# Two-layer graph network on one core: the normed inputs turned to channels by DMA, as planes of half words

## The chip, the cores and the metric

The kernel runs on one core of a Trainium2 chip. The metric is the device time of one execution in microseconds (us), the median of the runs shown; less is better. The engines are named as the profile names them: PE is TensorE (PEld its weight loads), DVE is VectorE, ACT is ScalarE, POOL is GpSimd, SP is the engine from which most DMAs are issued. "L312" is line 312 of the kernel before.

## What is computed

64 graphs of 256 nodes and 256 channels go through two residual layers, each with a layer norm and a ReLU ahead of it.

```python
# layer 0: three steps of message passing with one GRU cell
h = relu(layernorm(x))
A = (adj != 0)
for i in range(3):
    m = h @ weight[i]
    aggr = einsum('bst,bsd->btd', A, m)
    h = gru_cell(aggr, h, w_ih, w_hh, b_ih, b_hh)   # three gates of 256 channels
x = x + h
# layer 1: attention with 4 heads of 64 channels over the same graph
h = relu(layernorm(x))
v = h @ W.T + b
logits = leaky_relu(l_src[:, :, None, :] + l_dst[:, None, :, :], 0.2)
logits = where(adj == 1, logits, -9e15)
x = x + softmax(logits, axis=2) @ v
```

## The kernel before

**Tiling.** The graphs are taken in 32 pairs. A pair has 512 nodes, as four row tiles of 128 nodes (`R` = 4) by 256 channels (`D`). The state of layer 0 is kept with channels on the partitions: `hT_a` is 128 x (2 x 512), two halves of the channels (`KD` = 2) by 512 nodes. So the normed input `xn_a`, which has nodes on the partitions, has to be turned before layer 0, and `xn_b` before layer 1.

**How it is turned.** `plan_relu_T` (L360) does it for both layers: for each half of the channels PE transposes four 128 x 128 blocks against the identity into one PSUM bank (L370, tiles `pt_a` and `pt_b`), and ACT copies the bank out with a ReLU (L371). `plan_norm` (L329) makes `xn`: statistics on DVE (L339, L340), the inverse deviation on POOL (L346), and `xn` = (x - mean) * rstd on DVE (L351).

**The order of the work.** Nothing is scheduled by a planner that knows costs. Each piece of work is put by hand at a tick and one of three phases (STEP, READY, REST) with `at(tick, phase, pair, fn)`; the program is emitted tick by tick, phase by phase, the later pair first. Each engine then runs its own instructions strictly in that order. A step of the GRU takes 6 ticks (`SUB`); pair p starts at tick 18p (`APART`); its three steps stand at its ticks 0, 12 and 24. The gaps are filled by the steps of the neighbours, so that every stretch of 6 ticks holds one step of one pair. Over 18 ticks three such stretches follow each other and then repeat. They are called stages here, by the ticks modulo 18: stage B is ticks 0 to 5, stage C ticks 6 to 11, stage A ticks 12 to 17.

**Inside one step** (`Step`, L384) PE runs, in this order: `qa`, the sums over neighbours `pa` (L440), small blocks `qa`, `qb` (L418), and blocks of eight matmuls each (L312): `pc`, `p`, `pd`, `pc`, `pd`, `pe`, `pn`, `pd`, `pn`. DVE makes operands between them: L453, L461, L462, L468, L474, then L479 (writes `pe` from the first `pd`), L495 (`first_n`, writes the start of each of the two `pn` banks, on which PE then accumulates), L489 (reads the second `pd`, after which PE may add the third), and at the step's end, after POOL's L510, the new state with L527 and L528.

**Beside the steps** stand, at fixed ticks of each pair:

- `xn_a` (statistics at -14 and -13, result at -7), its turning at -4 and -3, and `hNhi_a`, `hNlo_a` (L742, L746), which split the ReLU of `xn_a` in two parts for the sums over neighbours;
- `edge` at -1 and `noedge` at 35 (L733, L800), made from the adjacency, `noedge` also written to DRAM;
- `xn_b` at 32 to 34, its turning at 35 and 36, the values `pv` (PE L820, DVE L824, which adds the bias `b_val`) at 37 and 38;
- `score_rows` (L853) at 39: a small transpose, four small DMAs to DRAM, and two loads `drow` that spread the scores over all partitions;
- `linked` (L863) at 36: a DMA transpose of `noedge` out of DRAM, issued on SP; from it ACT fills the logits `zz` (L872) at 38 to 41;
- `add_rows` (L878) at 43, 44 and 56, 57: DMAs issued on POOL that add rows onto `zz`;
- the row maxima (L899) at 43 to 50, the leaky ReLU on ACT (L919) at 48 to 55, the exponentials (L934) at 60 to 63, the products `po` (PE L542) with their division (DVE L551, L553) and residual (POOL L558) at 62 to 65, and the write of the result (L531) at 66.

SP issues, in order: the write of an old pair's result, the loads of x and of both uses of the adjacency, the small score rows, `drow`, `noedge` to DRAM, and `linked`. Buffers are rings by tag (`BUFS`, L100): a load waits until the old content of its buffer has been used.

Of the kernel before, what the change touches and what calls it, by code (L numbers as in the profile page):

```python
# [9 lines left out]
F32 = mybir.dt.float32  # L10
F32R = mybir.dt.float32r
BF16 = mybir.dt.bfloat16
I32 = mybir.dt.int32
AF = mybir.ActivationFunctionType
ALU = mybir.AluOpType
# [11 lines left out]
def gated_gnn_then_gat_kernel(  # L27
# [69 lines left out]
    def bank(name):  # L97
        return ps_m.tile([P, 512], F32, tag="mm", name=name)

    BUFS = {  # L100
        "x": 5, "adj": 2, "edge": 2, "noedge": 2, "hT_a": 2, "xn": 2, "val": 2, "row": 4, "zz": 4, "o": 2,
    }

    def buf(tag, shape, name, dtype=F32):
# [7 lines left out]
    def load_adj(p, name):  # L112
        at = buf("adj", [P, R, N], f"{name}_{p}", I32)
        nc.sync.dma_start(at, adj_rows[ts(p, T), :].rearrange("(r q) t -> q r t", q=P))
        return at

    def load_x(p):
        xt = buf("x", [P, R, D], f"x_{p}")
        nc.sync.dma_start(xt, x_rows[ts(p, T), :].rearrange("(r q) d -> q r d", q=P))
        return xt  # L120
# [13 lines left out]
    def load_square(tag, name, src):  # L134
        y = buf(tag, [P, KD, D], name)
        nc.sync.dma_start(y, src.rearrange("(k q) e -> q k e", q=P))
        return y
# [5 lines left out]
    hh_T = [buf("row", [P, G * P], f"hh_T_{k}") for k in range(KD)]  # L143
    w_msgs = [load_square("Z", "w_msg_0", weight[0])]
    ih_nat = load_gates("ih", w_ih)
    w_msgs += [load_square("row", f"w_msg_{l}", weight[l]) for l in range(1, L)]
    w_nat = load_square("zz", "w_nat", W)
    bi = const.tile([P, G], F32, name="bi")
    bh = const.tile([P, G], F32, name="bh")
# [176 lines left out]
    def at(tick, phase, p, fn):  # L326
        plan.setdefault(tick, ([], [], []))[phase].append((-p, fn))

    def plan_norm(src, name, p, ticks):  # L329

        v = {}

        def stats(r0):
            def fn():
                if not v:
                    v["st"] = small.tile([P, R, 6], F32, tag="st", name=f"st_{name}")
                    v["mv"] = small.tile([P, R, 2], F32, tag="mv", name=f"mv_{name}")
                for r in (r0, r0 + 1):
                    nc.vector.bn_stats(v["st"][:, r, :], src()[:, r, :])  # L339
                    nc.vector.bn_aggr(v["mv"][:, r, :], v["st"][:, r, :])  # L340
            return fn

        def deviation():
            rstd = v["rstd"] = small.tile([P, R], F32, tag="rstd", name=f"rstd_{name}")
            nc.vector.tensor_scalar_add(rstd, v["mv"][:, :, 1], EPS)
            nc.gpsimd.tensor_tensor(rstd, rstd, mhalf, ALU.pow)  # L346

        def result():
            xn = v["xn"] = buf("xn", [P, R, D], f"xn_{name}")
            for r in range(R):  # L350
                nc.vector.tensor_scalar(  # L351
                    xn[:, r, :], src()[:, r, :], v["mv"][:, r, 0:1], v["rstd"][:, r : r + 1],
                    op0=ALU.subtract, op1=ALU.mult,
                )

        for t, fn in zip(ticks, (stats(0), stats(2), deviation, result)):
            at(t, READY, p, fn)
        return v

    def plan_relu_T(v, tag, name, p, ticks):  # L360

        w = {}

        def fn(k):
            def go():
                if not w:
                    w["hT"] = buf(tag, [P, KD, T], f"hT_{name}")
                pt = bank(f"pt_{name}_{k}")
                for r in range(R):
                    nc.tensor.transpose(pt[:, ts(r, P)], v["xn"][:, r, ts(k, P)], ident)  # L370
                nc.scalar.activation(w["hT"][:, k, :], pt, AF.Relu)  # L371
            return go

        for k, t in enumerate(ticks):
            at(t, REST, p, fn(k))
        return w

    def by_c(y):
# [331 lines left out]
    def plan_pair(p):  # L710
# [5 lines left out]
        def ready(t, fn):  # L716
            at(t0 + t, READY, p, fn)
# [4 lines left out]
        def rest(t, fn):  # L722
            at(t0 + t, REST, p, fn)


        if p == 0:
            v["x"], v["adj"] = first
        else:
            rest(-20, lambda: v.update(x=load_x(p), adj=load_adj(p, "adj")))

        def to_edge():
            v["edge"] = buf("edge", [P, R, N], f"edge_{p}", F32R)
            nc.vector.tensor_scalar(v["edge"], v["adj"], 0.0, None, op0=ALU.not_equal)  # L733

        xn_a = plan_norm(lambda: v["x"], f"a{p}", p, [t0 - 14, t0 - 13, t0 - 13, t0 - 7])
        ready(-1 if p else -2.5, to_edge)
        h = plan_relu_T(xn_a, "hT_a", f"a{p}", p, [t0 - 4, t0 - 3])


        def first_hi():  # L740
# [66 lines left out]
        if last:  # L807
            plan_tail(t0, p, v, g, lambda i: turn_back(L - 1, i), residual)
            return
        xn_b = plan_norm(lambda: v["x"], f"b{p}", p, [t0 + 32, t0 + 33, t0 + 33, t0 + 34])  # L810
        hb = plan_relu_T(xn_b, "hT_b", f"b{p}", p, [t0 + 35, t0 + 36])

        def values(r0):
            def fn():
                if r0 == 0:
                    v["val"] = buf("val", [P, R, VW], f"val_{p}")
                for r in (r0, r0 + 1):
                    pt = bank(f"pv_{p}_{r}")
                    for k in range(KD):
                        nc.tensor.matmul(  # L820
                            pt[:, :VW], hb["hT"][:, k, ts(r, P)], w_val[:, k, :],
                            start=(k == 0), stop=(k == KD - 1),
                        )
                    nc.vector.tensor_add(v["val"][:, r, :], pt[:, :VW], b_val)  # L824
                if r0 == 0:
                    v["score"] = small.tile([P, R, 2 * H], F32, tag="score", name=f"score_{p}", bufs=2)
                nc.vector.tensor_copy(v["score"][:, r0 : r0 + 2, :], v["val"][:, r0 : r0 + 2, S0:])
            return fn

        rest(37, values(0))  # L830
        rest(38, values(2))

        def as_rows(src, n, what):

# [21 lines left out]
                drow[i] = buf("row", [P, H, N], f"drow_{p}_{i}")  # L856
                nc.sync.dma_start(drow[i].rearrange("q h n -> q (h n)"), on_all(rows["score"][i], H, 1)[:, 0, :])

        rest(39, score_rows)

# [5 lines left out]
        def barred_in(i, j):  # L868
            def fn():
                if j == 0:  # L870
                    logits[i] = buf("zz", [P, KN, H, N], f"zz_{p}_{i}")
                nc.scalar.activation(  # L872
                    logits[i][:, j, :, :], v["link"][:, j : j + 1, ts(i, N)].to_broadcast([P, H, N]),
                    AF.Identity, scale=1 / 16,
                )
            return fn

        def add_rows(i, what):  # L878
            def fn():
                nc.gpsimd.dma_start(  # L880
                    logits[i].rearrange("q j h n -> q j (h n)"), on_all(rows[what][i], 0, KN), accum_op=ALU.add
                )
            return fn

        rest(36, linked)
        ready(38, barred_in(0, 0))
        ready(39, barred_in(0, 1))
        ready(40, barred_in(1, 0))
        ready(41, barred_in(1, 1))
        rest(43, add_rows(0, "score"))  # L890
        rest(44, add_rows(1, "score"))

        def maxima(r, h0):
            def fn():
                if r == 0 and h0 == 0:
                    v["top"] = small.tile([P, R, H], F32, tag="top", name=f"top_{p}", bufs=2)
                for h in (h0, h0 + 1):
                    any_ = buf("any", [P, N], f"any_{p}_{r}_{h}")
                    nc.vector.tensor_tensor_reduce(  # L899
                        any_, drow[r // KN][:, h, :], v["noedge"][:, r, :], 1.0, -3.0e38, ALU.add, ALU.max,  # L900
                        accum_out=v["top"][:, r, h : h + 1],
                    )
            return fn
# [21 lines left out]

        for y in range(R * H // 2):
            r, h0 = divmod(2 * y, H)
            ready(43 + y if not late else 45 + (3 * y) // 8, maxima(r, h0))
            ready(48 + y if not late else 47 + r // KN, leaky(r, h0))
        ready(51 if not late else 47, shift)  # L930
        def exps(i, j):
            def fn():
                zz = logits[i][:, j, :, :]
# [9 lines left out]
        if late:  # L943
            left["rows", p] = shift_rows
            left["add", p] = lambda: [add_rows(i, "topT")() for i in range(PB)]
            for i in range(PB):
                left["exps", p, i] = lambda i=i: [exps(i, j)() for j in range(KN)]
        else:
            rest(52, shift_rows)
            rest(56, add_rows(0, "topT"))  # L950
            rest(57, add_rows(1, "topT"))
            for t, (i, j) in zip((60, 61, 62, 63), ((0, 0), (0, 1), (1, 0), (1, 1))):
                ready(t, exps(i, j))
        if p >= NPAIR - 3:
            for r in range(R):
                left["product", p, r] = lambda r=r: product(p, r, logits[r // KN], v, bank if late else gate_bank)
                left["divided", p, r] = lambda r=r: divided(p, r, v, nc.gpsimd.tensor_add)
            left["write", p] = lambda: write(p, v["x"], 0, R)
        else:
            for r, t in enumerate((62, 63, 64, 65)):  # L960
                rest(t, output(r))
            rest(66, lambda: write(p, v["x"], 0, R))

    for p in range(NPAIR):
        plan_pair(p)
# [52 lines left out]
```

## Time and profile before

| | |
|---|---|
| median of 3 runs | 2533.7 us (2533.55 to 2534.89) |
| profiled execution, its own time | 2540.86 us |
| its span | 2539.1 us |
| granted PE clock, mean | 0.995 |
| busy: PE, PEld, DVE, ACT, POOL | 2514.5, 2246.4, 1824.1, 1466.2, 645.5 us |

The profiled execution took 7.2 us more than the median. A pair takes about 77 us in the steady part (three stages); 32 pairs, a start and a tail make the span. In the lines of the timeline the first column is the start, the second the time from the start to the end of the group; an instruction's recorded duration overlaps its successor a little, so that costs in a row of instructions are best read from start to start.

### The profile page before, as it was taken

To read this page: it belongs to the slowest core of one execution; us is meant where nothing else is said; L and a number is where in the kernel's file an instruction comes from. 1 tells how busy PE (TensorE), PEld (TensorE's weight loads), DVE (VectorE), ACT (ScalarE), POOL (GpSimd) and SP (SyncE) were. 2 spreads that over 40 slices of the span, in tenths; PEclk is the share of its full clock that TensorE was granted. 3 is DMA by queue.
4 is the path that set the end of the run, shared out by engine and by line. 5 is a ranking of instruction groups with operands and counts; after the bars stand their busy time and mean duration, and the time that the engine had idled before them with its cause. 6 is when DMAs were issued, how large, how long until landed. Compare 5 with 4: busy or idle time off the path is not lost.

```text
span 2539.1 us, 38539 instructions
## 1 busy us (share of the span) xinstructions
PE 2514.5 (99%) x13918; PEld 2246.4 (88%) x13918; DVE 1824.1 (72%) x4458; ACT 1466.2 (58%) x3095; POOL 645.5 (25%) x514
## 2 busy tenths in 40 slices
PE   8999999999999999999999999999999999999998
PEld 6888898888889888989888988888988889898887
DVE  5567777677777777776777776777777777767667
ACT  3456565565555565555665655655656656556664
POOL 0122232222222222323232323222222223222221
PEclk9999999999999999999999999999999999999998
DMA  3033434553435544345544444534344544354443
GB/s 94 17 74 88 97 93 108 109 125 92 92 92 117 109 113 99 87 95 117 117 100 93 98 102 109 125 92 100 88 113 109 119 95 93 87 124 110 93 95 89
DMA packets 168223, 251.91 MB, mean 99 GB/s; under 512 B 42896, under 2 KB 128352, under 8 KB 168032
## 3 DMA queue, kind: packets, MB, share of 16 engines
q0 software_dynamic: 33728, 130.03, 26.6%
q1 hardware_dynamic: 132736, 119.41, 16.0%
q8 instruction: 110, 1.80, 0.3%
q14 instruction: 81, 0.66, 0.1%
q10 hardware_dynamic: 1568, 0.01, 0.0%
HBM read 215.62 MB, written 25.67 MB: 95 GB/s over the span
## 4 chain that ended last, share of the span: by engine, by line
PE 97%; DVE 1%; DMA 1%; ACT 1%; issue 0%; POOL 0%; SPq 0%; DVEq 0%
PE pd L312 20%; PE pn L312 13%; PE pc L312 13%; PE po L542 9%; PE pa L440 7%; PE qb L418 6%; PE pe L312 6%; PE p L312 6%; PE qa L418 5%; PE pv L820 4%; PE pback L770 3%; PE pt_a L370 1%; PE pt_b L370 1%; PE pc L238 1%; DVE any L899 0%; DMA hh_nat<-in_L_gnn_w_hh_dram 0%
## 5 line engine op out<-in xcount | busy, mean ns | idle before, releaser
L510 POOL TENSOR_TENSOR R<-hT_a,hn 128x512 f32<-128x512 f32 x191 | 317.8, 1664 | 879.4 <-ACT hn L506 821.5
L312 PE MATMUL pn<-aggr,w_a 128*128 128x256 f32 x1536 | 367.1, 382 | 0.0
L312 PE MATMUL pd<-T,w_a 128*128 128x256 f32 x1536 | 366.3, 381 | 0.0
L312 PEld LDWEIGHTS pn<-aggr,w_a 128*128 128x128 f32 x1536 | 287.0, 190 | 43.1 <-DVE pn L495 6.4
L312 PEld LDWEIGHTS pd<-T,w_a 128*128 128x128 f32 x1536 | 287.9, 191 | 37.6
L542 PEld LDWEIGHTS po<-val,zz 128*128 128x128 f32 x2048 | 250.3, 195 | 4.5
L542 PE MATMUL po<-val,zz 128*128 128x65 f32 x2048 | 247.2, 275 | 0.0
L899 DVE CUSTOM_DVE_ANT_0 any<-drow,noedge 128x256 f32<-128x256 f32 x496 | 236.9, 478 | 9.8 <-DMA drow<-score_dram 1.0
L506 ACT ACTIVATE hn<-pn,bi 128x256 f32<-128x256 f32 x384 | 160.3, 469 | 144.3 <-PE pn L312 144.2
L425 ACT ACTIVATE R<-pc,brz 128x256 f32<-128x256 f32 x192 | 80.5, 470 | 278.5 <-PE pc L312 278.5
L527 DVE SCALAR_TENSOR_TENSOR R<-Z,R 128x512 f32<-128x512 f32 x192 | 131.8, 687 | 147.6 <-POOL R L510 142.8
L558 POOL TENSOR_TENSOR x<-x,o 128x256 f32<-128x256 f32 x124 | 112.0, 904 | 481.6 <-DVE o L553 481.6
L761 DVE TENSOR_TENSOR hNlo<-pback,hNhi 128x512 fp32r<-128x512 f32 x128 | 88.4, 691 | 201.6 <-ACT hNhi L760 201.6
L919 ACT ACTIVATE zz<-zz,val 128x256 f32<-128x256 f32 x496 | 224.9, 509 | 0.0
L495 DVE SCALAR_TENSOR_TENSOR pn<-R,hn 128x512 f32<-128x512 f32 x192 | 142.5, 742 | 93.7 <-ACT hn L421 77.2
L425 ACT ACTIVATE R<-pe,brz 128x256 f32<-128x256 f32 x192 | 80.5, 470 | 185.9 <-PE pe L312 185.9
L528 DVE SCALAR_TENSOR_TENSOR hT_a<-R,hn 128x512 f32<-128x512 f32 x192 | 174.6, 909 | 14.3 <-ACT m5n L446 1.4
L312 PE MATMUL pd<-T,w_h 128*128 128x256 f32 x768 | 181.5, 379 | 0.0
L312 PE MATMUL pc<-aggr,w_a 128*128 128x256 f32 x768 | 181.5, 379 | 0.0
L312 PE MATMUL pe<-aggr,w_a 128*128 128x256 f32 x768 | 181.4, 379 | 0.0
L312 PE MATMUL pc<-hT_a,w_h 128*128 128x256 f32 x768 | 181.4, 379 | 0.0
L312 PE MATMUL p<-T,w_a 128*128 128x256 f32 x768 | 181.4, 379 | 0.0
(176 smaller groups left out, 5258.5 us busy)
## 6 DMA issues: line engine op xcount, KB each, us to landing
zz<-score_dram POOLq DMA_DIRECT2D x62, 1024.0 KB, 11.7
zz<-topT_dram POOLq DMA_DIRECT2D x62, 1024.0 KB, 8.7
adj<-in_adj_dram SPq DMA_DIRECT2D x64, 512.0 KB
drow<-score_dram SPq DMA_DIRECT2D x62, 512.0 KB
x<-in_x_dram SPq DMA_DIRECT2D x32, 512.0 KB
out_dram<-x SPq DMA_DIRECT2D x31, 512.0 KB
noedge_dram<-noedge SPq DMA_DIRECT2D x31, 256.0 KB
score_dram<-score SPq DMA_DIRECT2D x124, 4.0 KB
```

The source lines that it names most:

```text
L312: nc.tensor.matmul(pt[:, ts(c, N)], w[:, k, j * D + c * P : j * D + (c + 1) * P], src[:, k, :], start=start and c == 0 and k == 0, stop=(c ...
L418: nc.tensor.matmul(pt, w_n[:, j, :], src, start=start, stop=True, skip_group_check=True)
L425: nc.scalar.activation(of(dst, i)[:, c, :], src[:, c, :], AF.Tanh, bias=brz[:, g0 + c : g0 + c + 1], scale=0.5)
L440: nc.tensor.matmul(pt[:, ts(i, N)], hN[half][:, i * KN + s, ts(e, P)], edge[:, i * KN + s, :], start=(s == 0 and half == 0), stop=(s == KN ...
L495: nc.vector.scalar_tensor_tensor(by_c(self.bank(f"pn{i}")), of(self.R, i), 1.0, of(self.hn, i), op0=ALU.add, op1=ALU.mult)
L506: nc.scalar.activation(n__[:, c, :], p_n[:, c, :], AF.Tanh, bias=bi[:, 2 * KD + c : 2 * KD + c + 1])
L510: nc.gpsimd.tensor_sub(of(self.R, i), of(self.hT(), i), n__)
L527: nc.vector.scalar_tensor_tensor(d_, of(self.Z, i), 1.0, d_, op0=ALU.add, op1=ALU.mult)
L528: nc.vector.scalar_tensor_tensor(of(self.hT(), i), d_, 0.5, of(self.hn, i), op0=ALU.mult, op1=ALU.add)
L542: nc.tensor.matmul(po[:, ts(h_, VC)], zz[:, j, h_, ts(s, P)], v["val"][:, i * KN + j, ts(h_, VC)], start=(j == 0), stop=(j == KN - 1),)
L899: nc.vector.tensor_tensor_reduce(any_, drow[r // KN][:, h, :], v["noedge"][:, r, :], 1.0, -3.0e38, ALU.add, ALU.max, accum_out=v["top"][:, ...
L919: nc.scalar.activation(zz[:, h, :], zz[:, h, :], AF.Prelu, alpha=ALPHA, bias=v["val"][:, r, S0 + H + h : S0 + H + h + 1],)
```

## The change

Instead of PE and ACT, the DMA engines turn the normed inputs: for layer 0 of the pairs from 2 on, for layer 1 of the pairs 0 to 28. The first pairs, and layer 1 of the last three, keep the old way.

The new `plan_turn` has three parts. `halve` (DVE) copies the 128 x 1024 values as 128 x 2048 half words so that the low and the high half words of a row lie in separate planes (`words`), and SP writes the 512 KB to DRAM. `turn` (SP) reads them back with a DMA transpose of 2-byte elements into `turned`. `join` (DVE) puts the two half words of each value together again in `hT_a` or `hT_b`.

The ReLU has to come ahead of that. For layer 0 ACT applies it to `xn_a` in place. For layer 1 `plan_norm` makes `xn_b` = max(x - mean, 0) without the factor, and the factor `rstd` is multiplied in where the values leave PSUM.

Some ticks move: layer 0's `xn_a` is made at -10 rather than -7, and everything of layer 1 from the values on stands 6 ticks (`later`) later. The loads of x and adjacency go from -20 to -16, and the ring `row` has 2 buffers in place of 4.

```diff
+    def plan_turn(src, tag, name, p, ticks):
+        w = {}
+        def halve():
+            words = buf("words", [P, R, 2, D], f"words_{name}", U16)
+            nc.vector.tensor_copy(words.rearrange("q r w d -> q r d w"), src().bitcast(U16).rearrange("q r (d w) -> q r d w", w=2))
+            w["rows"] = dram.tile([R, P, 2 * D], U16, tag="words", name=f"words_dram_{name}")
+            nc.sync.dma_start(w["rows"].rearrange("r q e -> q r e"), words.rearrange("q r w d -> q r (w d)"))
+        def turn():
+            w["turned"] = buf("turned", [P, 2, KD * T], f"turned_{name}", U16)
+            nc.sync.dma_start_transpose(
+                w["turned"].rearrange("q w (k n) -> q (w k) n", k=KD), w["rows"].rearrange("r q e -> (r q) e")
+            )
+        def join():
+            w["hT"] = buf(tag, [P, KD, T], f"hT_{name}")
+            nc.vector.tensor_copy(
+                flat(w["hT"]).bitcast(U16).rearrange("q (n w) -> q n w", w=2), w["turned"].rearrange("q w n -> q n w")
+            )
+        at(ticks[0], READY, p, halve)
+        at(ticks[1], REST, p, turn)
+        at(ticks[2], READY, p, join)
+        return w
...
-        "x": 5, "adj": 2, "edge": 2, "noedge": 2, "hT_a": 2, "xn": 2, "val": 2, "row": 4, "zz": 4, "o": 2,
+        "x": 5, "adj": 2, "edge": 2, "noedge": 2, "hT_a": 2, "xn": 2, "val": 2, "row": 2, "zz": 4, "o": 2,
...
-            rest(-20, lambda: v.update(x=load_x(p), adj=load_adj(p, "adj")))
+            rest(-16, lambda: v.update(x=load_x(p), adj=load_adj(p, "adj")))
...
-        h = plan_relu_T(xn_a, "hT_a", f"a{p}", p, [t0 - 4, t0 - 3])
+        if dma_a:
+            ready(-10, lambda: nc.scalar.activation(flat(xn_a["xn"]), flat(xn_a["xn"]), AF.Relu))
+            h = plan_turn(lambda: xn_a["xn"], "hT_a", f"a{p}", p, [t0 - 9, t0 - 8, t0 - 3])
+        else:
+            h = plan_relu_T(xn_a, "hT_a", f"a{p}", p, [t0 - 4, t0 - 3])
...
+        dma_b = p < NPAIR - 3
+        later = SUB if dma_b else 0
+        xn_b = plan_norm(lambda: v["x"], f"b{p}", p, [t0 + 32, t0 + 33, t0 + 33, t0 + 34], dma_b)
+        if dma_b:
+            hb = plan_turn(lambda: xn_b["xn"], "hT_b", f"b{p}", p, [t0 + 34.1, t0 + 35, t0 + 41])
+        else:
+            hb = plan_relu_T(xn_b, "hT_b", f"b{p}", p, [t0 + 35, t0 + 36])
...
-                    nc.vector.tensor_add(v["val"][:, r, :], pt[:, :VW], b_val)
+                    if dma_b:
+                        nc.vector.scalar_tensor_tensor(
+                            v["val"][:, r, :], pt[:, :VW], xn_b["rstd"][:, r : r + 1], b_val,
+                            op0=ALU.mult, op1=ALU.add,
+                        )
+                    else:
+                        nc.vector.tensor_add(v["val"][:, r, :], pt[:, :VW], b_val)
...
-        rest(37, values(0))
-        rest(38, values(2))
+        rest(37 + later, values(0))
+        rest(38 + later, values(2))
...
-        rest(36, linked)
-        ready(38, barred_in(0, 0))
+        rest(37 if dma_b else 36, linked)
+        ready(38 + later, barred_in(0, 0))
```

The score rows, `add_rows`, maxima, leaky ReLU, exponentials, products and the write get the same `+ later`.

More of the change, by code (lines that the diff above doesn't have):

```diff
@@ L12 @@
 BF16 = mybir.dt.bfloat16
+U16 = mybir.dt.uint16
 I32 = mybir.dt.int32
@@ L145, in gated_gnn_then_gat_kernel @@
     ih_nat = load_gates("ih", w_ih)
-    w_msgs += [load_square("row", f"w_msg_{l}", weight[l]) for l in range(1, L)]
+    w_msgs += [load_square("noedge", f"w_msg_{l}", weight[l]) for l in range(1, L)]
     w_nat = load_square("zz", "w_nat", W)
@@ L327, in at, with plan_norm @@
         plan.setdefault(tick, ([], [], []))[phase].append((-p, fn))
-    def plan_norm(src, name, p, ticks):
+    def plan_norm(src, name, p, ticks, relu=False):
         v = {}
@@ L351, in result @@
                 nc.vector.tensor_scalar(
-                    xn[:, r, :], src()[:, r, :], v["mv"][:, r, 0:1], v["rstd"][:, r : r + 1],
-                    op0=ALU.subtract, op1=ALU.mult,
+                    xn[:, r, :], src()[:, r, :], v["mv"][:, r, 0:1], 0.0 if relu else v["rstd"][:, r : r + 1],
+                    op0=ALU.subtract, op1=ALU.max if relu else ALU.mult,
                 )
@@ L733, in to_edge @@
             nc.vector.tensor_scalar(v["edge"], v["adj"], 0.0, None, op0=ALU.not_equal)
-        xn_a = plan_norm(lambda: v["x"], f"a{p}", p, [t0 - 14, t0 - 13, t0 - 13, t0 - 7])
+        dma_a = p >= 2
+        norm_ticks = (-14, -13, -13, -10) if dma_a else (-14, -13, -13, -7)
+        xn_a = plan_norm(lambda: v["x"], f"a{p}", p, [t0 + t for t in norm_ticks])
         ready(-1 if p else -2.5, to_edge)
-        h = plan_relu_T(xn_a, "hT_a", f"a{p}", p, [t0 - 4, t0 - 3])
+        if dma_a:
[3 more added lines that the diff above has]
+            h = plan_relu_T(xn_a, "hT_a", f"a{p}", p, [t0 - 4, t0 - 3])
         def first_hi():
@@ L809, in plan_pair @@
             return
-        xn_b = plan_norm(lambda: v["x"], f"b{p}", p, [t0 + 32, t0 + 33, t0 + 33, t0 + 34])
-        hb = plan_relu_T(xn_b, "hT_b", f"b{p}", p, [t0 + 35, t0 + 36])
+        dma_b = p < NPAIR - 3
[5 more added lines that the diff above has]
+            hb = plan_relu_T(xn_b, "hT_b", f"b{p}", p, [t0 + 35, t0 + 36])
         def values(r0):
@@ L857, in score_rows @@
                 nc.sync.dma_start(drow[i].rearrange("q h n -> q (h n)"), on_all(rows["score"][i], H, 1)[:, 0, :])
-        rest(39, score_rows)
+        rest(39 + later, score_rows)
         def linked():
@@ L883, in add_rows @@
             return fn
-        rest(36, linked)
-        ready(38, barred_in(0, 0))
[L887 to L891, printed above, removed]
+        rest(37 if dma_b else 36, linked)
+        ready(38 + later, barred_in(0, 0))
+        ready(39 + later, barred_in(0, 1))
+        ready(40 + later, barred_in(1, 0))
+        ready(41 + later, barred_in(1, 1))
+        rest(43 + later, add_rows(0, "score"))
+        rest(44 + later, add_rows(1, "score"))
         def maxima(r, h0):
@@ L927, in plan_pair @@
             r, h0 = divmod(2 * y, H)
-            ready(43 + y if not late else 45 + (3 * y) // 8, maxima(r, h0))
-            ready(48 + y if not late else 47 + r // KN, leaky(r, h0))
-        ready(51 if not late else 47, shift)
+            ready(43 + later + y if not late else 45 + (3 * y) // 8, maxima(r, h0))
+            ready(48 + later + y if not late else 47 + r // KN, leaky(r, h0))
+        ready(51 + later if not late else 47, shift)
         def exps(i, j):
@@ L948, in plan_pair @@
         else:
-            rest(52, shift_rows)
-            rest(56, add_rows(0, "topT"))
-            rest(57, add_rows(1, "topT"))
+            rest(52 + later, shift_rows)
+            rest(56 + later, add_rows(0, "topT"))
+            rest(57 + later, add_rows(1, "topT"))
             for t, (i, j) in zip((60, 61, 62, 63), ((0, 0), (0, 1), (1, 0), (1, 1))):
-                ready(t, exps(i, j))
+                ready(t + later, exps(i, j))
         if p >= NPAIR - 3:
@@ L960, in plan_pair @@
             for r, t in enumerate((62, 63, 64, 65)):
-                rest(t, output(r))
-            rest(66, lambda: write(p, v["x"], 0, R))
+                rest(t + later, output(r))
+            rest(66 + later, lambda: write(p, v["x"], 0, R))
     for p in range(NPAIR):
```

## The prediction

> **What bounds the kernel now.** I read the page first: busy time, then the chain that ended last.
>
> ```profile
> PE 2514.5 (99%) x13918; PEld 2246.4 (88%) x13918; DVE 1824.1 (72%) x4458; ACT 1466.2 (58%) x3095; POOL 645.5 (25%) x514
> ...
> PE 97%; DVE 1%; DMA 1%; ACT 1%; issue 0%; POOL 0%; SPq 0%; DVEq 0%
> ```
>
> PE is the bound: every other engine's work lies beside it. So PE work that disappears is worth its full time, as long as no other engine comes late to PE. An average of 72% does not tell that of DVE; one period of three stages does (windows: the stretch, its length, the busy us of PE, PEld, DVE, ACT and POOL, granted clock, DMA share, GB/s).
>
> ```profile
> 1199.78:1222.69 22.91, 22.91 (x125) 20.30 (x125) 20.43 (x53) 14.28 (x33) 5.19 (x4) 1.00 0.20 59
> 1222.69:1248.21 25.52, 25.52 (x134) 22.49 (x132) 16.33 (x36) 15.76 (x34) 5.86 (x5) 1.00 0.75 175
> 1248.21:1276.73 28.52, 28.52 (x176) 26.18 (x174) 19.41 (x49) 15.48 (x30) 9.60 (x9) 1.00 0.39 75
> ```
>
> These are stages A, B and C. PE fills each; DVE is at 89% of A, 64% of B and 68% of C.
>
> **What is removed.** The timeline of PE shows one turned half, four transposes:
>
> ```profile
> 1208.23 0.60 PE L370 MATMUL pt_a<-ident,xn_a 128*128 128x128 f32 x4
> 1208.66 0.60 PE L770 MATMUL pback<-ident,hT_a 128*128 128x128 f32 x4
> ```
>
> From start to start it costs 0.43 us. A turned input has two halves, 0.865 us. It is 30 inputs of layer 0 and 29 of layer 1: 59 x 0.865 = **51.0 us** off PE, 1.73 us a period. ACT's two copies of 0.6 us per input go too; layer 0 gets one ReLU of 128x1024 in place (like L742, 1.06 us). ACT is at 54 to 62% in all stages, so that counts nothing.
>
> **What is moved.** Values, scores, maxima, products and the rest of layer 1 stand one stage later. PE's sum stays, but its parts change stage. A loses three halves (1.30) and the small `ptopT` (0.11) and gains four products of 1.73: 28.4 us. B loses one half and the values (3.62): about 21.5. C loses the products and gains the values: about 25.3.
>
> DVE's parts move as well, and they go into the stage that was fullest: A gains two more ticks of maxima (0.93 each), four divisions (L551 and L553, 0.63 each) and two copies, one `join` of layer 0 and one `halve` of layer 1; it loses the small ends of the maxima (0.84 with L839).
>
> **What is added on DVE.** No row shows a copy of 128x2048 half words. The bounds come from these rows of the DVE timeline of A:
>
> ```profile
> 1211.44 0.69 DVE L479 TENSOR_TENSOR pe<-pd,m 128x512 f32<-128x512 f32 x1
> ...
> 1214.57 1.23 DVE L746 SCALAR_TENSOR_TENSOR hNlo_a<-xn_a,hNhi_a 128x1024 fp32r<-128x1024 f32 x1 [0.61 <-ACT hNhi_a L742]
> ...
> 1219.52 0.68 DVE L733 TENSOR_SCALAR edge<-adj 128x1024 fp32r<-128x1024 int32 x1
> ...
> 1221.39 0.67 DVE L800 TENSOR_SCALAR noedge<-adj 128x1024 bf16<-128x1024 int32 x1
> ```
>
> With one tensor from SBUF, 1024 elements take 0.68 us (L733, L800); with two, 1.23 (L746). For 2048 that is 1.2 or 2.3 us a copy. The copy has one tensor and lies in SBUF on both sides, so it is nearest to L733: I take 1.2, and keep 2.3 for the range. No row of DVE moves elements faster than L733 and L800 do, so 1.2 is also the lower end.
>
> [...]
>
> **Does DVE still keep up in A?** By sums: 20.4 + 1.9 + 2.5 + 2.4 - 0.8 = 26.4 us of work in 28.4. The order decides, and the tight piece is from L479 to the second L495, on which PE's last `pn` waits. From the end of the `pd` that L479 reads, PE has ahead of that `pn`: `pc` 1.73, a product 1.73, `qb` 0.43, `pd` 1.73, `pe` 1.73, a product 1.73, `pn` 1.73, `pd` 1.73, that is 12.54 us. DVE has, in the changed kernel's order, start to start: a lag of 0.2, L479 0.61, `join`, statistics 1.28, maxima 0.93, L746 1.15, a division 0.63, L495 0.61, L489 0.60, `xn_b` 1.29, maxima 0.93, a division 0.63, `halve`, L495 0.70. Without the copies this is 9.56 us; with two of 1.2 it is 11.96.
>
> To that comes what POOL costs DVE. DVE and POOL hold each other up, as these lines of DVE and POOL in C show:
>
> ```profile
> 1270.59 0.69 DVE L495 SCALAR_TENSOR_TENSOR pn<-R,hn 128x512 f32<-128x512 f32 x1
> 1271.19 1.79 DVE L351 TENSOR_SCALAR xn_a<-x,mv_a,rstd_a 128x256 f32<-128x256 f32 x4
> ```
>
> ```profile
> 1270.75 1.10 POOL L558 TENSOR_TENSOR x<-x,o 128x256 f32<-128x256 f32 x1 [5.02 <-DVE o L553]
> ```
>
> The four L351 take 1.79 beside POOL's add, 1.37 without it in A (1217.43). The products, now in A, bring these adds there: I take 0.35 for the one ahead of `xn_b`, and 0.7 (L558 undisturbed is 0.73) for the one that waits out `halve` and then stands in front of L495. So DVE needs about 13.0 us of 12.54: PE waits 0.45 us. Behind that A hands over late to B: L453 has about 0.7 us to spare at the start of A now (it ends 5.1 us into A, and the `qb` behind it starts at 5.85), and comes some 0.5 to 1 us later at the start of B then; I take 0.2 us of waiting, between 0 and 0.8. In C `halve` of layer 0 stands ahead of L495 with 0.85 us left at 1.2 us a copy: nothing, and 0.3 if it takes 2.3. Sum: 0.65 us for each of about 28 full periods, **18 us** given back.
>
> **The DMAs.** Per input 512 KB go to DRAM and come back. The nearest row is `linked`: its issue holds SP 1.24 us, and ACT waited for it in 6 of 31 cases, 4.6 us in all; the 256 KB moved within the two microseconds behind the issue. Twice that is about 3 us, and 5 to 10 beside POOL's adds onto `zz`. On SP the turn of layer 0 stands behind `drow`: `halve` about 15 us into C, turn issued near 21, landed some 3 us into A, and `join` is due at 13. The turn of layer 1 is issued at the end of A and due near 19 us into B; the write, `linked` and the loads of x and adjacency queue behind it, but SP waits for POOL's last add there anyway, and x lands about 6 us ahead of its statistics. These waits, the smaller ring `row`, and the factor in L824 (from 427 ns towards L468's 476, four a period, in C) I cost at nothing: that cover is 6 to 10 us deep, and each microsecond beyond it would cost 28.
>
> **The sum.** 51 - 18 = 33 us off the profiled execution (2540.9), so off the median too (the two differ by 0.3%, which is nothing on 33): 2533.7 - 33, about **2501**.
>
> **Rivals.** About 0.2%, 5 us, is what a measurement of this kernel can tell from no change.
>
> *All hidden* (10%). POOL's adds fall elsewhere and DVE fits: the full 51 us, 2483. For it: the bare sum 11.96 is under 12.54. Against it: in A nothing is left over.
>
> *DVE becomes the bound of A, at one element at a time* (30%). Copies of 2.3: A waits 2.65, B 0.5, C 0.3, together 3.4 a period, 96 us against 51: +44, 2578. It turns into a loss once the waits pass 1.73 + 0.1 a period, which is copies of 1.8 us. For it: nothing in the trace shows half words with a stride moving fast. It can grow by PE's clock:
>
> ```profile
> 2485.22 0.28 PE L837 MATMUL ptopT<-ident,top 128*16 128x128 f32 x1 [1.51 <-DVE top L910]
> ```
>
> After this gap of 1.51 us the granted clock was 0.69, 0.50, 0.50 and 0.61 in the next four stretches of 5 us, 8.5 us lost once. Waits of 2.6 us in each A might repeat some of that, up to 238 us; I give that a few per cent inside this case. [...]
>
> *Copies in between, 1.6 to 1.9* (15%). 2515 to 2540, on both sides of no change.
>
> *A turn lands late* (7%). Layer 0's turn shares the DMA engines with the adds onto `zz`, which run about 4 to 15 us into A: `join` at 15 rather than 13, 2 us a period, +56 on 2501: 2557.
>
> **The numbers.** The forecast itself, 38%, lies from 2487 to 2525. Faster: 38 + 10 and 2 of the in-between, 50%. Within 0.2%: 9. Slower: 30 + 7 and 4, 41%. The range 2484 to 2585 leaves out a little below and the clock's part above.
>
> **What would show it.** Right: no `pt_a`, `pt_b` in the steady part, copies near 1.2 us, PE at 99% with waits on DVE's `pn` (L495) of about 0.5 us once a period. Wrong: copies of 2 us or more, waits of PE on `pn` of over 1.7 us in A, half clock in the steady part, or DVE waiting for `turned`.

## The result and the profile after

The changed kernel takes 2834.64 us (median of 4 runs, 2820.63 to 2836.93) against 2534.06 us of the kernel before in the same comparison (2533.55 to 2534.89): the ratio is 1.1174, with a 95% interval of 1.1138 to 1.1211. The forecast was 2501 and the range ended at 2585. The profiled execution has a span of 2831.7 us, 292.6 more than before; the medians differ by 300.6, since the profiled execution before was above its median. Line numbers from here on are those of the kernel that is named; in the changed kernel `halve` is L387, `join` L399, `first_n` (L495 before) L525, the first operand after `pd` (L479 before) L509, POOL's residual (L558 before) L588.

The page of the changed kernel, busy times and the chain that ended last by engine and by line:

```profile
PE 2582.9 (91%) x13446; PEld 2259.8 (80%) x13446; DVE 2161.0 (76%) x4576; ACT 1440.8 (51%) x3007; POOL 763.6 (27%) x514
...
PE 65%; DVE 26%; ACT 5%; issue 2%; POOL 1%; DMA 1%; DVEq 0%; SPq 0%; ACTq 0%; POOLq 0%
PE pd L313 12%; PE pn L313 12%; PE pc L313 9%; PE po L572 7%; DVE words_a L387 6%; PE pa L470 5%; DVE words_b L387 5%; PE qb L448 4%; PE qa L448 4%; PE p L313 4%; PE pe L313 4%; PE pback L807 2%; DVE pn L525 2%; DVE val L868 2%; DVE hNlo L798 2%
```

Before, the chain was 97% PE. Now a quarter of it is DVE, and the two copies of `halve` alone are 11%. PE has 472 matmuls less and is nevertheless busy 68.4 us longer; that is the second thing to explain. The groups of the four copies (busy us, mean ns of one, then idle time before them):

```profile
L387 DVE COPY words_a<-xn_a 128x2048 uint16<-128x2048 uint16 x30 | 161.6, 5388 | 0.0
L387 DVE COPY words_b<-xn_b 128x2048 uint16<-128x2048 uint16 x29 | 154.9, 5343 | 0.0
...
L399 DVE COPY hT_a<-turned_a 128x2048 uint16<-128x2048 uint16 x30 | 36.5, 1218 | 0.0
L399 DVE COPY hT_b<-turned_b 128x2048 uint16<-128x2048 uint16 x29 | 36.5, 1259 | 0.0
```

`join`, which reads from two planes by turns and writes in one piece, takes 1.22 us, as forecast. `halve`, which reads in one piece and writes to two planes by turns, takes 5.35. Both move the same 2048 half words a partition. DVE has no wait for `turned` in 59 joins: the DMAs are hidden. What PE waits for, from the waits of PE (us in total, times, longest):

```profile
PE pn L313 <- DVE pn L525: 208.5, 61, 5.5
PE qb L448 <- DVE qb L483: 9.1, 12, 0.8
PE pscore L886 <- DVE score L876: 7.3, 29, 0.8
```

That is about 3.4 us twice in a period, once in stage C and once in stage A. In C it is the first L525 that comes late (lines of DVE and PE, start, us; between the two lines of DVE stand four short steps):

```profile
1241.32 5.33 DVE L387 COPY words_a<-xn_a 128x2048 uint16<-128x2048 uint16 x1
1247.84 0.68 DVE L525 SCALAR_TENSOR_TENSOR pn<-R,hn 128x512 f32<-128x512 f32 x1
```

```profile
1248.57 3.64 PE L313 MATMUL pn<-aggr,w_a 128*128 128x256 f32 x8 [3.38 <-DVE pn L525]
```

In A it is the second, by the timelines of DVE, POOL and PE:

```profile
1277.92 5.40 DVE L387 COPY words_b<-xn_b 128x2048 uint16<-128x2048 uint16 x1
1282.73 1.57 DVE L525 SCALAR_TENSOR_TENSOR pn<-R,hn 128x512 f32<-128x512 f32 x1
1284.22 1.75 DVE L763 TENSOR_SCALAR edge<-adj 128x1024 fp32r<-128x1024 int32 x1
```

```profile
1278.08 5.66 POOL L588 TENSOR_TENSOR x<-x,o 128x256 f32<-128x256 f32 x1 [3.07 <-DVE o L583]
1283.70 1.71 POOL L540 TENSOR_TENSOR R<-hT_a,hn 128x512 f32<-128x512 f32 x1
```

```profile
1278.87 1.89 PE L313 MATMUL pd<-T,w_a 128*128 128x256 f32 x8
1284.35 3.78 PE L313 MATMUL pn<-aggr,w_a 128*128 128x256 f32 x8 [3.59 <-DVE pn L525]
```

In A `halve` holds the second L525 back, as the prediction's tight piece says it would if it were too long. POOL's add of 0.7 us ends only when `halve` has ended (5.66), and the POOL instructions that have piled up behind it then stand beside L525 and `edge`, which take 1.57 and 1.75 us instead of 0.69 and 0.68. (With the short `halve` of e1 below they take 1.22 and 1.76 at this place, so most of that is not due to its length.) And the eight matmuls behind the gap take 3.78 instead of 1.89 us. The windows behind this gap show why (stretch, length, busy us of PE, PEld, DVE, ACT, POOL, granted clock, DMA share, GB/s):

```profile
1284.35:1288.00 3.65, 3.65 (x9) 2.93 (x10) 3.65 (x6) 0.00 (x0) 1.07 (x1) 0.50 0.41 139
1288.00:1292.00 4.00, 4.00 (x28) 3.95 (x27) 1.79 (x7) 1.20 (x3) 1.76 (x2) 0.79 0.88 188
```

After this gap the granted clock is a half. With the first experiment below, which runs the same matmuls at a granted clock of 0.998, the 292.6 us come apart into three terms: PE's busy time is 2469.2 there, so the missing transposes give -45.3, the half clock +113.7 (2582.9 - 2469.2), and PE's idle time (span less busy, 248.8 against 24.6) +224.2. The clock records agree with the second term: they hold 243.5 us of half clock against 14.4 in e1, and half of the difference is 114.6. The first term holds some clock too, since the profile before has 26.9 us of half clock: about 6 of the 45.3 us.

### The profile page after: what moved, and what is told of

It reads as the page before. It is cut to its first block, busy times and chain, and to the rows that moved or that the text cites. A ratio compares the mean times of both kernels' runs of the same rounds, so it can differ in the third digit from the quotient of the medians.

```text
span 2831.7 us, 37693 instructions
## 1 busy us (share of the span) xinstructions
PE 2582.9 (91%) x13446; PEld 2259.8 (80%) x13446; DVE 2161.0 (76%) x4576; ACT 1440.8 (51%) x3007; POOL 763.6 (27%) x514
## 4 chain that ended last, share of the span: by engine, by line
PE 65%; DVE 26%; ACT 5%; issue 2%; POOL 1%; DMA 1%; DVEq 0%; SPq 0%; ACTq 0%; POOLq 0%
PE pd L313 12%; PE pn L313 12%; PE pc L313 9%; PE po L572 7%; DVE words_a L387 6%; PE pa L470 5%; DVE words_b L387 5%; PE qb L448 4%; PE qa L448 4%; PE p L313 4%; PE pe L313 4%; PE pback L807 2%; DVE pn L525 2%; DVE val L868 2%; DVE hNlo L798 2%
## 5 line engine op out<-in xcount | busy, mean ns | idle before, releaser
L540 POOL TENSOR_TENSOR R<-hT_a,hn 128x512 f32<-128x512 f32 x191 | 294.5, 1543 | 1436.4 <-ACT hn L536 1344.6
L313 PE MATMUL pn<-aggr,w_a 128*128 128x256 f32 x1536 | 444.4, 441 | 208.5 <-DVE pn L525 208.5
L313 PEld LDWEIGHTS pn<-aggr,w_a 128*128 128x128 f32 x1536 | 328.0, 221 | 287.0 <-DVE pn L525 233.3
L313 PE MATMUL pd<-T,w_a 128*128 128x256 f32 x1536 | 377.3, 390 | 0.0
L588 POOL TENSOR_TENSOR x<-x,o 128x256 f32<-128x256 f32 x124 | 255.0, 2057 | 384.8 <-DVE o L583 384.8
L313 PEld LDWEIGHTS pd<-T,w_a 128*128 128x128 f32 x1536 | 299.1, 198 | 43.2
L572 PEld LDWEIGHTS po<-val,zz 128*128 128x128 f32 x2048 | 257.9, 200 | 6.0
L948 DVE CUSTOM_DVE_ANT_0 any<-drow,noedge 128x256 f32<-128x256 f32 x496 | 220.8, 445 | 9.6 <-DMA drow<-score_dram 0.8
L525 DVE SCALAR_TENSOR_TENSOR pn<-R,hn 128x512 f32<-128x512 f32 x192 | 155.5, 810 | 19.0 <-ACT hn L451 10.9
L313 PEld LDWEIGHTS pd<-T,w_h 128*128 128x128 f32 x768 | 142.2, 190 | 26.4 <-DVE pe L509 8.9
```

What stands on the lines that cost most here:

```text
L313: nc.tensor.matmul(pt[:, ts(c, N)], w[:, k, j * D + c * P : j * D + (c + 1) * P], src[:, k, :], start=start and c == 0 and k == 0, stop=(c ...
L525: nc.vector.scalar_tensor_tensor(by_c(self.bank(f"pn{i}")), of(self.R, i), 1.0, of(self.hn, i), op0=ALU.add, op1=ALU.mult)
L540: nc.gpsimd.tensor_sub(of(self.R, i), of(self.hT(), i), n__)
L572: nc.tensor.matmul(po[:, ts(h_, VC)], zz[:, j, h_, ts(s, P)], v["val"][:, i * KN + j, ts(h_, VC)], start=(j == 0), stop=(j == KN - 1),)
L588: add(v["x"][:, r, :], v["x"][:, r, :], o)
L948: nc.vector.tensor_tensor_reduce(any_, drow[r // KN][:, h, :], v["noedge"][:, r, :], 1.0, -3.0e38, ALU.add, ALU.max, accum_out=v["top"][:, ...
```

## The experiments

The theory after the result: everything comes from the way in which `halve` writes; its time holds L525 back, the second in A and the first in C, and the gaps set off the half clock. Rivals: the moves of ticks and loads; DVE's whole added work, in whatever form; the place of `halve` rather than its time.

**1. Written plane by plane (e1).** One line; the same bytes in the same places, and now the read steps 4 bytes:

```diff
-nc.vector.tensor_copy(words.rearrange("q r w d -> q r d w"), half.rearrange("q r (d w) -> q r d w", w=2))
+nc.vector.tensor_copy(words, half.rearrange("q r (d w) -> q r w d", w=2))
```

(`half` is `src().bitcast(U16)` in all these excerpts.)

> The same halve, but the copy walks plane by plane: it writes 256 neighbouring half words in a row and reads every second half word, where the changed kernel writes to the two planes in turn and reads neighbours. Theory 1 (the changed kernel's loss is the write that hops between planes at every half word, 5.35 us a copy against 1.22 for join): the copy falls to 1.2 to 1.3 us, PE's waits on L525 from 3.4 us to under 0.7, the granted clock back to 0.99, and the time to the sum of the prediction, 2485 to 2520. Rival (the moves by one stage, the DMAs and the crowding of DVE and POOL in stage A cost as much): the copy is quick, but the time stays above 2534. Second rival (a copy of half words with a stride is slow whichever side has the stride): the copy stays above 4 us and the time near 2830.

Measured: 2521.78 us, ratio 0.9946 (0.9927 to 0.9965). So with the order of the two loops turned round the changed kernel is faster than the kernel before. The groups and the longest repeated waits of this kernel:

```profile
L387 DVE COPY words_a<-xn_a 128x2048 uint16<-128x2048 uint16 x30 | 36.5, 1217 | 0.0
L387 DVE COPY words_b<-xn_b 128x2048 uint16<-128x2048 uint16 x29 | 35.3, 1217 | 0.0
```

```profile
PE qb L448 <- DVE qb L483: 16.8, 28, 0.7
PE pscore L886 <- DVE score L876: 7.2, 29, 0.8
PE pn L313 <- DVE pn L525: 1.7, 2, 1.5
```

The wait on `pn` is gone, and what is left of DVE's lateness in A shows at the hand-over to B (`qb`, 0.6 us a period).

**2. Layer 0 alone by DMA (e2)**, with `halve` as in the change; layer 1 keeps its transposes and its ticks (`dma_b = False`).

> Only layer 0 is turned by DMA, with the slow halve; layer 1 is turned by PE and stands where it stood before. Theory 1, with the place deciding the price: halve stands in stage C ahead of L525, where the products are back and leave DVE about 4.4 us (L495 ran at 1265.28 in the kernel before, the pn behind it at 1269.76), so 5.35 us cost about 1 us of waiting, no half clock; join costs about 0.5 us in A; against 26 us off PE the time is 2535 to 2560. Rival (each halve costs the same wherever it stands): half of the 300 us, near 2680.

Measured: 2650.04 us, ratio 1.0444 (1.041 to 1.0479), nearer to the rival. My expectation counted on slack in C that is not there: PE waits 92.8 us on `pn`, in the steady part about 2.4 us at a time behind `halve` where I had 1. One slow copy a period in C already costs several times what the transposes of its layer did.

**3. The moves alone (e3)**: values and the rest of layer 1 a step later, the loads at -16, the ring `row` with 2 buffers, and the old transposes.

> Nothing is turned by DMA: PE turns both layers as before, but everything of layer 1 from the values on stands 6 ticks later, with the earlier loads and the smaller ring as in the changed kernel. Theory 1: the moves cost little, 2530 to 2545. Rival (crowding of stage A by the moves): a good part of the 300 us, over 2600.

Measured: 2534.25 us, ratio 0.9996 (0.9985 to 1.0007). The moves cost nothing; that rival is out.

**4. `halve` in four pieces over two ticks (e5)**, written as in the change.

> The slow halve in four copies of one row tile each, spread over the next two ticks, and the turn behind the last. Theory 1 with the clock: the DVE time is the same (about 1.35 us a copy, 5.4 an input), but no single wait of PE is over 1.5 us, so the granted clock stays at 0.99 and only waits are left, 1 to 2.5 us a period: 2530 to 2600. Rival (DVE's time as such is the bound, however it is cut): within 40 us of the changed kernel, over 2790.

Measured: 2766.76 us, ratio 1.0904 (1.0875 to 1.0934), between the two and nearer to the rival. The pieces take 1.5 us each, and PE's waits move:

```profile
PE qb L456 <- DVE qb L491: 128.2, 29, 4.5
PE pn L313 <- DVE pn L533: 36.9, 55, 2.0
```

L525 (L533 here) now holds PE for 0.7 us at a time, but the same work then is late at the start of B, once a period. Spread over two ticks, the time is paid at another place: what costs is the time, and not only where it stood.

**5. Both halves on ACT (e4)**, plane by plane (`nc.scalar.copy`).

> Both halves are made on ACT instead of DVE, read 4 bytes apart and written plane by plane. Theory (the rest of the gain that e1 did not bring stands in DVE's queue at the end of stage A, the PE wait on qb of 0.6 us a period and the 0.23 us on score): DVE loses 2 x 1.2 us a period, both waits go, 28 x 0.83 = 23 us off 2521.8, so 2495 to 2505. ACT's copies cost about 2.0 us each (1024 elements take 1.06 us, 512 take 0.59). Rival (ACT is late instead: in A the copy stands ahead of the ACT step hn on pn, and ACT has 1.9 us free there): a wait of PE of 0.5 to 1 us a period on an ACT line takes its place, 2515 to 2540.

Measured: 2515.3 us, ratio 0.9921 (0.9906 to 0.9935). ACT needs 1.90 us a copy. The waits on `qb` are gone, but PE now waits 0.33 us a period on L525, which waits for ACT: the rival's mechanism, in C rather than in A.

**6. Layer 0's halves on DVE, layer 1's on ACT (e8)**, both plane by plane:

```diff
+planes = half.rearrange("q r (d w) -> q r w d", w=2)
+if name.startswith("a"):
+    nc.vector.tensor_copy(words, planes)
+else:
+    nc.scalar.copy(words, planes)
```

> As e1, but layer 1's halve (the one at the end of stage A) on ACT; layer 0's stays on DVE. Theory (e1's wait on qb at the start of B comes from the tight end of A alone): the qb wait goes, 28 x 0.6 = 17 us off, 2500 to 2510, at or a little behind the kernel with both on ACT. Rival (ACT late in A, ahead of hn on pn): 2515 to 2540, and then the kernel with both on ACT is no better.

Measured: 2498.03 us, ratio 0.9852 (0.9835 to 0.9868), the best kernel here that leaves nothing out. Its page:

```profile
PE 2462.4 (99%) x13446; PEld 2186.6 (88%) x13446; DVE 1889.9 (76%) x4547; ACT 1487.0 (60%) x3036; POOL 611.4 (24%) x514
```

PE is the bound again. So e1's remaining wait did come from the tight end of A, and ACT had the 1.9 us there.

**7. Half of the row tiles by turns (e6)**, the other half plane by plane, to tell the stall from the clock.

> Of the four row tiles two are written hopping between the planes as in the change, two plane by plane: 2.67 + 0.61 = 3.3 us a halve, and the PE gaps of 3.4 us that the change has twice a period become about 1.4 us. It separates the stall from the clock. Theory (the clock is halved only after gaps longer than about 3 us): half clock stays at e1's 14 us, and the time is 2521.8 + 28 x 2 x 1.4 less the 0.6 that is in e1 already, about 2580 (2565 to 2600). Rival (a gap of 1.5 us is enough, as the tail of the kernel before suggests): each gap brings some us of half clock, over 100 us of it in all, 2640 to 2700.

Measured: 2686.47 us, ratio 1.0588 (1.0568 to 1.0608). The gaps are 1.55 us in C and 2.65 in A, where POOL's piled-up work adds a microsecond (the second `pn` write, L527 here, takes 1.75 us instead of 0.69). The windows behind the one and the other:

```profile
930.70:934.10 3.40, 3.40 (x16) 3.01 (x17) 1.13 (x2) 2.02 (x5) 0.39 (x1) 1.00 0.47 156
963.85:967.15 3.30, 3.30 (x8) 2.64 (x9) 3.17 (x9) 0.00 (x0) 0.00 (x0) 0.50 0.24 82
```

After 1.55 us the clock stays whole; after 2.65 it is a half for the next 3.41 us, in all steady periods but one. Neither theory had it: the time is in the rival's range, but not because gaps of 1.5 us halve the clock. A's gap was long enough because it did not shrink to the 1.4 us that I had expected.

**8. One row tile of four by turns (e12).**

> One row tile of four is written hopping, three plane by plane: 1.35 + 0.95 = 2.3 us a halve, which is the upper bound that the prediction took for a copy. The prediction's sum for copies of 2.3 us was 2578 with the joins at that price too; the joins are 1.2 here. By the gaps of e6 (1.56 in C, 2.65 in A) less the 1.1 us that each copy gets shorter: 0.45 and 1.55 us, no half clock, and 28 x (2.0 + 0.23 + 0.5 for starting up - 1.2 that e1 has) = 43 on 2522, about 2565 (2550 to 2580). Rival (a gap of 1.55 us in A halves the clock as 2.65 does, 1.7 us a period): 2600 to 2625.

Measured: 2587.81 us, ratio 1.0208 (1.0191 to 1.0225), and a granted clock of 0.998: gaps of 1.33 and 1.17 us halve nothing. But the dose was not the one intended:

```profile
893.88 1.50 DVE L388 COPY words_a<-xn_a 128x512 uint16<-128x512 uint16 x1
894.92 2.05 DVE L389 COPY words_a<-xn_a 128x1536 uint16<-128x1536 uint16 x1
896.88 0.68 DVE L436 TENSOR_TENSOR T<-hT_a 128x512 f32<-128x512 f32 x1
```

From start to start the two pieces take 3.0 us, not 2.3, because the three row tiles plane by plane take 1.96, more than four take in e1. Why three take longer than four is not shown.

**9. The factor left out (e10)**, so that layer 1's values are not those of the reference.

> As e8, but the factor rstd of layer 1's values is left out: DVE adds the bias only, 0.43 us instead of 0.49 for each of four a period. Theory (PE's wait of 0.23 us a period on score in stage C comes from the factor): the wait goes, and 28 x (0.23 + about 0.15 for starting up again) = about 10 us off 2498, so 2486 to 2492. Rival (the wait comes from the values' new place, and two steps 0.06 us shorter do not end it): over half of the wait stays, 2494 to 2498.

Measured: 2490.57 us, ratio 0.9825 (0.981 to 0.9839), 7.5 us below e8. PE's wait on `score` falls from 7.5 us in 29 times to 1.1 us in 2: it came from the factor.

**10. What of the writing costs so much (e7, e9, e13, e11).** Three kernels put an extra copy ahead of e1's, which writes over it; one makes layer 1's halve on ACT with the change's order. They were run once each, for their rows.

> An extra copy of the same half words stands ahead of e1's copy, which writes over it: for layer 0 one whose writes are 4 bytes apart without changing planes, for layer 1 one that changes planes at each half word with the planes 2 KiB apart instead of 512 B. Only the durations of the rows are wanted. Theory (changing the region at every half word costs, a step does not): 1.2 us for layer 0, 5.3 us for layer 1. Rival 1 (any output that is not contiguous costs): 4 to 5.4 us for both. Rival 2 (the distance matters): layer 1 well off 5.3, say under 3.5 or over 7. The kernel's time: 2620 to 2720 if layer 0's extra copy takes 1.2 us, near the change's own 2835 if it takes 5.

> An extra copy of the same 4 KB a partition stands ahead of e1's copy, which writes over it; only the durations of the rows are wanted. For layer 0 it moves 1024 elements of 4 bytes and changes between two planes 2 KiB apart at each; for layer 1 it moves 2048 half words, two to a plane before it changes, so 1024 changes too. Theory 1 (a price for each change of plane, 5.34 us / 2048 = 2.6 ns): 2.7 us for both. Theory 2 (a price for each half word that is not written together with its neighbour): about 0.7 to 1.2 us for layer 0 and 1.2 us for layer 1. Theory 3 (one price for each element once the output hops): 2.7 us for layer 0, 5.3 us for layer 1.

> An extra copy stands ahead of e1's copy, which writes over it; only the durations of the rows are wanted. For layer 0: 1024 half words, from plane to plane at each, 2 KiB apart, each into 4 bytes of its own. For layer 1: 2048 half words, from plane to plane at each as in the change, the planes 32 bytes apart. Theory A (slow is that the two halves of one 4-byte word are written with a write elsewhere between them): layer 0 about 1.1 us, as 1024 elements of 4 bytes took, and layer 1 about 5.3 us. Theory B (slow is each change of plane by a half word): layer 0 2.7 us, layer 1 5.3. Theory C (slow is the change to a far line): layer 0 2.7 us, layer 1 1.2 to 2.

> As e8, but layer 1's halve on ACT is written as the change writes it, from plane to plane at each half word. Theory (the price belongs to DVE's way of writing): ACT takes 1.9 us as it does plane by plane, and the time is e8's 2498 within 5 us. Rival (it is the memory's price, whichever engine writes): about 5.3 us on ACT, which then is late with hn on pn at the end of A: PE waits some 3 us a period, 2580 or more.

The groups of the extra copies, of e7, of e9 and of e13 (layer 0's in the line with `words_a`, layer 1's with `words_b`):

```profile
L394 DVE COPY words_b<-xn_b 128x2048 uint16<-128x2048 uint16 x29 | 154.9, 5343 | 0.0
...
L389 DVE COPY words_a<-xn_a 128x2048 uint16<-128x2048 uint16 x30 | 41.3, 1378 | 0.0
```

```profile
L389 DVE COPY words_a<-xn_a 128x1024 f32<-128x1024 f32 x30 | 34.1, 1136 | 0.0
L394 DVE COPY words_b<-xn_b 128x2048 uint16<-128x2048 uint16 x29 | 31.8, 1096 | 0.0
```

```profile
L395 DVE COPY words_b<-xn_b 128x2048 uint16<-128x2048 uint16 x29 | 143.0, 4929 | 0.0
L390 DVE COPY words_a<-xn_a 128x1024 uint16<-128x1024 uint16 x30 | 83.1, 2771 | 0.0
```

Half words written 4 bytes apart in one direction: 1.38 us, so a step is not what costs. By turns to planes 2 KiB apart: 5.34, to planes 512 B apart (the change): 5.35, to planes 32 B apart: 4.93, so the distance hardly matters. 1024 half words by turns, each in 4 bytes of its own: 2.77, the same price for each, so it is not that two halves of a word are written apart. 4-byte elements by turns, or half words two at a time: 1.1 us for 1024 changes. So of the theories written down ahead, the one with a price for each change of plane by a single half word (2.4 to 2.7 ns) fits all rows, and a change with 4 bytes costs 1.1 ns at the most, the time of the element included. Why a half word alone is dearer than a 4-byte element stays open. The kernels took 2777.67 (e7), 2577.83 (e9) and 2786.78 us (e13).

On ACT (e11, 2623.82 us) the same order is dearer still, 9.38 us against 1.90 plane by plane in e4 and e8, so the price isn't DVE's alone (the lines of e8 and of e11):

```profile
L391 ACT COPY words_b<-xn_b 128x2048 uint16<-128x2048 uint16 x29 | 55.0, 1898 | 1.6 <-DVE xn_b L353 1.6
```

```profile
L390 ACT COPY words_b<-xn_b 128x2048 uint16<-128x2048 uint16 x29 | 271.9, 9376 | 1.6 <-DVE xn_b L353 1.6
```

## Why the prediction was wrong, step by step

*The step that failed is the price of `halve`.* The prediction had no row for a copy of half words, took 1.2 us because the copy is "nearest to L733", and bounded it from above with L746, 2.3 us. It measured 5.35. The rows that it leaned on all write in one piece; they could bound the read side and the number of elements, and for `join` they did (1.2 forecast, 1.22 measured), but not a write that changes planes. The upper bound was therefore no bound, and the range fell with it. The case in between, copies of 1.6 to 1.9 us, had no row either. "Wrong: copies of 2 us or more" was the right thing to look for in the profile.

*What PE loses by the transposes was right.* 51.0 us were forecast, 1.73 a period. From start to start the transposes take 60.9 us of PE in e3, which keeps them all, and 9.4 in e8: 51.5 are gone. PE's busy time fell by less: by 36.5 us in e1 and 43.3 in e8 against e3's 2505.7, which has the same half clock as they (14 to 15 us). The 45.3 and 52.1 against the profile before are larger because that profile had more half clock. What comes back, some 8 us in e8, is in part start-up behind waits, and the rest isn't traced. A gap costs somewhat more than its own length: a group of eight matmuls ends 0.16 us after the start of the next one in the unbroken stream.

*The moves in themselves cost nothing*, as forecast (e3).

*The tight piece in A was the right place, its balance not quite.* With copies of 1.22 us (e1) the forecast was a wait of 0.45 us on `pn` in A and 0.2 at the hand-over to B, 0.65 a period. Measured: hardly any on `pn` and 0.6 on `qb` at the hand-over. POOL's contention falls where the prediction put it, on what follows `halve` (1.22 us for L525 and 1.76 for `edge` in e1, instead of 0.69 and 0.68). So 2501 was missed by e1, at 2521.8: the waits come to 0.9 us with 0.23 on `score`, instead of 0.65, and to about 0.16 for starting up behind each of the two gaps. That is 0.55 a period, 15 of the 21 us; the rest is of the size of what PE's busy time got back (above), and isn't traced to lines.

*The factor in L824 was not free.* "I cost at nothing" was wrong by 7.5 us (e10). DVE's four steps are only 0.06 us longer each, but in C nothing covers them ahead of `score`.

*The DMAs are hidden*, as forecast: no DVE wait on `turned` in the changed kernel or in e1.

*The rival had the mechanism but too small a price.* "DVE becomes the bound of A" is what happened, in C as well. It put copies of 2.3 us at 2578. With `halve` at 3.0 and `join` at 1.2 the time is 2587.8 (e12). Worked out for these sizes, the rival's sum gives 2.25 us of waiting in A, 0.5 in B and 0.95 in C, about 2587; measured are gaps of 1.17 in A, none in B and 1.33 in C, so that the total agrees in part by luck. From there to the changed kernel's `halve` of 4.9 us from start to start the gaps grow to about 3.5 in A and 3.4 in C: each further microsecond of `halve` costs PE somewhat more than a microsecond at each place.

*The clock was given a few per cent, and it is 113.7 of the 292.6 us.* The row that I feared it from misled in its figure: behind the same gap of 1.50 us in the tail of e1 the clock stays at 1.00, and gaps of about 1.5 us in e6 and e9 halve nothing. The expectation of e6 has about 3 us as the least gap that halves the clock; no run shows that limit: gaps of 2.17 us in e11 and 2.65 us in e6 were enough in 12 and in 27 of 28 cases (below). Nor does every longer gap cost the clock: in the changed kernel it was halved behind 46 of the 59 gaps of 3.1 to 5.5 us.

## What to carry to other kernels

Where a copy takes half words apart or puts them together, let the reading side jump and the writing side run in one piece: turning round the order of the loops alone took this change from 11.7% slower to 0.5% faster, and a place with room for one of the copies, on ACT, to 1.5% faster. A row bounds an operation's cost only if it has the same pattern on the side that may be slow; where no row writes like that, keep the upper end open and measure the copy by itself first. And where PE is the bound, a wait can cost twice, once as the stall and once as the clock: here half clock followed 12 of 28 gaps of 2.17 us (e11) and 27 of 28 of 2.65 us (e6), and each 3.41 us of it cost about 1.7 us more.

## What the runs showed of the hardware that was not expected

- A change of plane at each half word costs 2.4 to 2.7 ns on DVE's output, nearly the same for planes 32 B, 512 B and 2 KiB apart, and at most 1.1 ns with 4 bytes at a time. An input read by turns (`join`, 1.22 us for 2048 half words) costs no more than one read 4 bytes apart (e1, 1.22). ACT pays 4.6 ns (9.38 us for 2048).
- POOL's add waits such a copy out: 5.66 us beside it, where an undisturbed one takes 0.7.
- Gaps of PE of about 1.5 us left the clock whole (e6, e9, e12). After gaps of 2.17 us in e11 it was halved 12 times of 28, after 2.3 us in e13 once of 28, after 2.4 us in e2 16 times of 28, after 2.65 us in e6 27 times of 28. So the length alone does not decide. The windows behind three of e11's gaps, one with half clock and two without:

```profile
1033.86:1037.20 3.34, 3.34 (x17) 2.93 (x18) 3.20 (x4) 2.01 (x5) 2.56 (x2) 1.00 0.71 154
1113.60:1117.50 3.90, 3.90 (x11) 3.14 (x12) 3.76 (x5) 1.94 (x5) 2.47 (x2) 0.56 0.81 190
1193.23:1196.60 3.37, 3.37 (x17) 2.96 (x18) 3.23 (x4) 2.01 (x5) 2.54 (x2) 1.00 0.73 150
```

  The halved stretches in the traces' clock records last 3.41 us or a multiple (the last one of a trace can be cut off by its end). In each of the 15 traces all of them start on one grid of 3.413 us, to within 5 ns. With PE's rows cut at this grid (windows at full clock, without the first 100 us and the last window), half clock followed in 201 of 201 windows in which PE was idle for 2.03 us or more, in 3 of 7 with 1.95 to 2.03 us, and in 4 of 265 with 1.0 to 1.95 us (those four had about 1.5 us and stood near the start or the end of a kernel). The trace of the changed kernel alone has 46 of 46, 1 of 4 and 0 of 25. So in these traces half clock went with where a gap lay on this grid, not with its length alone. The second of the three gaps above lies whole in one window; the first and the third are cut in two by its border, with 1.67 and 1.55 us in the larger part.
